# Row maxima written into score banks by ScalarE, and a new division of denominators, rotation and output projection, in a one-core macaron block

## The chip, the core and the metric

The kernel runs on one core of a Trainium2 chip. The metric is the device time of one execution in microseconds (us). The core's engines run side by side and wait for one another by semaphores: TensorE (PE, with its weight loads PEld), VectorE (DVE), ScalarE (ACT), GpSimd (POOL) and SyncE (SP), whose queue issues the DMAs here. Matmuls write to PSUM, of which the kernel uses eight banks of 128 x 512 fp32 numbers; everything else lies in SBUF or in device memory.

## What is computed

Three residual steps on x of 4 x 1024 tokens and 128 features:

```python
x = x + 0.5 * ffn(layernorm(x))      # 8 routed experts of width 128, silu(gate) * up
x = x + attn(layernorm(x))           # attn has its own layernorm and its own residual
x = x + 0.5 * ffn(layernorm(x))
```

The change lies in the attention, which has 16 heads of 64 and goes through latents of 64 numbers:

```python
c_q, c_kv = h @ w_down_q.T, h @ w_down_kv.T
q, k, v = heads(c_q @ w_up_q.T), heads(c_kv @ w_up_k.T), heads(c_kv @ w_up_v.T)
q, k = rope(q), rope(k)              # even' = even*cos - odd*sin, odd' = even*sin + odd*cos
attn = softmax(q @ k.T / 8)          # over 1024 keys, for 4 batches and 16 heads
out = concat_heads(attn @ v) @ w_out.T + residual
```

## The kernel before, in words

**Units, groups and slots.** Two heads are worked on together, one (hh = 0) in rows 0 to 63 of the PE array and one (hh = 1) in rows 64 to 127; the two form two streams of matmuls that run side by side. A unit U is one pair of heads, one half of the queries (512) and all 1024 keys, which are 8 slots of 128 keys. There are 64 units or 512 slots. The program walks over them in 128 groups g of four slots, so a unit is an even group and the odd one after it, a "pair" below.

**What a group does on PE.** First come the rows: `rows(hh)` yields for each stream 16 score matmuls (`score`, L781) and, between them, three of the four matmuls of the maxima (`passA`, L755) at the steps that `MAXIMA` lists, stream 0 first and stream 1 second. They are written alternately, one of each stream. After the rows follow the side work and the fourth maximum (before the side work in stream 1, after it in stream 0). In even groups the side work is the rotation's matmuls (L647, three in each stream), in odd groups the output projection (L839, four in each stream). Even groups then have the denominator of the unit before (`den`, L816). Last come the values of the four slots of the group before (`values`, L804, 16 column-split matmuls into psC).

**Scores.** Operands are kept in two parts (a rounded one and its remainder), so a slot of one stream takes three matmuls. A fourth, the row matmul, multiplies a row of ones by `maxr`, one row of negated row maxima, and so subtracts the maximum of every query. ACT then writes exp(0.125 x) into p (L785), and POOL sums the p of a unit into acc (L797). The last p of a unit can be left out of acc; `direct(U)` says how many, and `den` multiplies these with ones on PE as parts of their own, besides the part that acc is. It copies the bank to dsb (L818, ACT), which goes through device memory to dT.

**Banks.** psA[0] and psA[1] take the maxima of the two streams, psC the values. The scores go through psS[0..3] and psX in turn: slot s of stream hh uses number (2 (s mod 4) + hh) mod 5. The rotation and the output projection use psX and psS[3]; `den` and the layernorm's transposes take psS[0] and psS[1] by `aux`.

**Maxima.** A maximum's matmul runs 15 slots ahead of its use and is reduced by DVE from its one bank of 128 x 512 (L756). Once 16 of a unit are there, L760 negates and joins them, and `max_row` sends them through device memory (d) into `maxr`, in the middle of the group's rows: two DMAs on SP, the second after the first has landed.

**Rotation.** `rope(..., "vector")` (L660 to L664) runs on DVE in 55 even groups: a 1024-wide product from PSUM into rt, two 512-wide products within PSUM, two 512-wide additions into eo. ACT rounds eo into hi_r in the next odd group (L672, "cast"), and POOL takes the remainder (L680).

**Output projection.** In an odd group, three groups after its denominator, `outp` multiplies osb with G (w_up_v and w_out joined) into two banks. ACT scales the first bank in place, four times 128 wide (L849); DVE adds the scaled second bank to X, four times (L852), and then the first, 512 wide (L854).

**What sets the order.** All of it is an order written out by hand: each engine runs its instructions in the order in which this program issues them, and `at(g, fn, place)` puts a step off to a later group, at "side", "mid" (in the rows) or "end". Background work (layernorm, router) fills places called `step`. `direct`, `MAXIMA` and the dictionary of the rotation's places are the planner's constants.

Of the kernel before, what the change touches and what calls it, by code (L numbers as in the profile page):

```python
# [28 lines left out]
NSLOT = B * 128  # L29
NGRP = NSLOT // 4  # L30
PBUFS = 8
MAXIMA = ((3, 8, 13), (0, 5, 10))
OTHER, VECTOR, PE, NEVER = 0, 1, 2, 3
NROPE = 9
ACTS = (4, 6, 7)
# [5 lines left out]

def direct(U):

    return 1 if U % 3 == 2 and U < 56 else 0


class Kernel:
# [10 lines left out]
    def setup(self):  # L58
# [34 lines left out]
        for hh in range(2):  # L93
            nc.gpsimd.memset(self.f(self.one_row[64 * hh:64 * hh + 1, :]), 1.0)
        self.maxr = [const.tile([128, 512], F32R, name=f"maxr{i}") for i in range(2)]
        for t in self.maxr:
            nc.gpsimd.memset(self.f(t), 0.0)

# [12 lines left out]
    def aux(self):  # L111

        self.nrest += 1
        return self.rest[(self.nrest - 1) % len(self.rest)]

    def router_weights(self):
        nc, wrf = self.nc, self.wrf
# [507 lines left out]
    def rope(self, n, stage):  # L625
# [14 lines left out]
        elif stage == "mm":  # L640
            ps = w["ps"] = self.rope_banks
            hi, lo = w["C"][:, 0, :], w["C"][:, 1, :]

            def mm(k, eo):
                wt, c = ((self.wup1, hi), (self.wup1, lo), (self.wup2, hi))[k]
                r64 = slice(64 * eo, 64 * eo + 64)
                nc.tensor.matmul(ps[eo], wt[r64, qk * 4 + g, :], c[r64, :], start=k == 0, stop=k == 2)  # L647
# [3 lines left out]
        elif stage in ("o", "e"):  # L651
            k = "eo".index(stage)
            ps = w["ps"][k].unsqueeze(1).to_broadcast([128, 2, 512])
            nc.vector.tensor_tensor(self.rt[:, 2 * k:2 * k + 2, :], ps, self.table[:, 1 - k:3 - k, cs], ALU.mult)
        elif stage == "vector":


            w["eo"] = P.tile([128, 2, 512], F32, name="eo", bufs=2)
            (even, odd), rt = w["ps"], self.rt
            nc.vector.tensor_tensor(rt[:, 0:2, :], even.unsqueeze(1).to_broadcast([128, 2, 512]), self.table[:, 1:3, cs], ALU.mult)  # L660
            nc.vector.tensor_tensor(even, odd, self.table[:, 0, cs], ALU.mult)
            nc.vector.tensor_tensor(odd, odd, self.table[:, 1, cs], ALU.mult)
            nc.vector.tensor_tensor(w["eo"][:, 1, :], odd, rt[:, 1, :], ALU.add)  # L663
            nc.vector.tensor_tensor(w["eo"][:, 0, :], even, rt[:, 0, :], ALU.add)  # L664
        elif stage == "sum":
            w["eo"] = P.tile([128, 2, 512], F32, name="eo", bufs=2)
            nc.gpsimd.tensor_tensor(w["eo"], self.rt[:, 0:2, :], self.rt[:, 2:4, :], ALU.add)  # L667
        elif stage in ("hi0", "hi1"):
            k = int(stage[2])
            if k == 0:  # L670
                w["hi"] = P.tile([128, 2, 512], F32R, name="hi_r")
            nc.scalar.copy(w["hi"][:, k, :], w["eo"][:, k, :])  # L672
        elif stage == "dhi":
            self.dma(out=scr[0:2, :, :, cs].rearrange("s h i t -> (h i) s t"), in_=w["hi"])
        elif stage in ("lo0", "lo1"):
            k = int(stage[2])
            eo = w["eo"][:, k, :]
            nc.gpsimd.tensor_tensor(eo.bitcast(F32R), eo, self.f(w["hi"][:, k, :]), ALU.subtract)
        elif stage == "lo":
            nc.gpsimd.tensor_tensor(w["eo"].bitcast(F32R), w["eo"], self.f(w["hi"]), ALU.subtract)  # L680
        elif stage == "dlo":
            self.dma(out=scr[2:4, :, :, cs].rearrange("s h i t -> (h i) s t"), in_=w["eo"])
            self.roped.add((b, g, qk, h))
            del self.rope_of[n]
# [78 lines left out]
    def max_row(self, U, m):  # L763
        nc = self.nc
        d = self.dram.tile([128, 8], F32, name=f"d3_{U % 4}")
        self.dma(out=d, in_=m)
        self.dma(out=self.maxr[U % 2][0:128:64, :].rearrange("h (q p) -> h q p", p=128), in_=d.rearrange("p (h q) -> h q p", h=2))

    def score(self, s, hh, k):

# [5 lines left out]
        ks = slice(c * 128, c * 128 + 128)  # L776
        r = slice(64 * hh, 64 * hh + 64)
        Q, K = self.QT[P % 3], self.KT[P % 3]
        ps = (self.psS + [self.psX])[(2 * (s % 4) + hh) % 5]
        w, x = ((K[r, 0, ks], Q[r, 0, qs]), (K[r, 0, ks], Q[r, 1, qs]), (K[r, 1, ks], Q[r, 0, qs]), (self.one_row[r, :], self.maxr[U % 2][r, :]))[k]  # L780
        nc.tensor.matmul(ps, w, x, start=k == 0, stop=k == 3)  # L781
        if k == 3:
            if hh == 0:
                self.p_of[s] = self.pp.tile([128, 2, 512], F32, name="p")
            nc.scalar.activation(self.p_of[s][:, hh, :], ps, AF.Exp, scale=0.125)  # L785
            if hh == 1:
                self.accumulate(s)

    def accumulate(self, s):
# [18 lines left out]
    def den(self, U):  # L808

        nc = self.nc  # L810
        osb = self.osb_of[U] = self.op2.tile([128, 512], F32, name="osb")
        pd = self.aux()
        parts = [self.p_of[8 * U + c] for c in range(8 - direct(U), 8)] + [self.acc_of[U]]
        for k, part in enumerate(parts):
            for n in range(4):
                nc.tensor.matmul(pd[32 * n:32 * n + 32, 0:256], self.ones, part[:, n // 2, 256 * (n % 2):256 * (n % 2) + 256], start=k == 0, stop=k == direct(U))  # L816
        dsb = self.op1.tile([128, 256], F32, name="dsb")
        nc.scalar.copy(dsb, pd[:, 0:256])  # L818
        dT = self.ms.tile([128, 8], F32, name="dT")
# [7 lines left out]
    def outp(self, U, osb, dT):  # L827
# [8 lines left out]

        def mm(i, hh):
            r = slice(64 * hh, 64 * hh + 64)
            nc.tensor.matmul(po[hh][:, i * 128:(i + 1) * 128], osb[r, i * 128:(i + 1) * 128], self.G[r, j, :], start=True, stop=True)  # L839

        for hh in range(2):
            self.halves[hh] += [lambda i=i, hh=hh: mm(i, hh) for i in range(4)]
# [1 line left out]
        def add():  # L844

            t0 = b * TPB + 4 * half
            for i in range(4):
                c = slice(i * 128, (i + 1) * 128)
                nc.scalar.activation(po[0][:, c], po[0][:, c], AF.Identity, scale=rT[:, i:i + 1])  # L849
            for i in range(4):  # L850
                x = self.X[:, t0 + i, :]
                nc.vector.scalar_tensor_tensor(x, po[1][:, i * 128:(i + 1) * 128], rT[:, 4 + i:5 + i], x, ALU.mult, ALU.add)  # L852
            x = self.X[:, t0:t0 + 4, :]
            nc.vector.tensor_tensor(x, po[0].rearrange("p (t d) -> p t d", t=4), x, ALU.add)  # L854

        self.at(self.group, add)

    def run(self):
# [109 lines left out]
        for _ in streams[2].pop() if streams[2] else ():  # L968
            pass
        assert not (streams[0] or streams[2])  # L970
        self.rest, self.rope_banks, self.bankO = self.psS[:2], [self.psX, self.psS[3]], [self.psX, self.psS[3]]
        streams[2] += [self.attn_pre(b) for b in range(1, B)]
        turns = {"next": 0}
        needs = {}
# [43 lines left out]
        for g in range(NGRP + 1):  # L1018
# [6 lines left out]

            def rows(hh):
                maxima = lambda i: self.passA(s0 + AHEAD + i, hh) if s0 + AHEAD + i < NSLOT else None
                for n in range(16):
                    if n in MAXIMA[hh]:
                        yield lambda n=n: maxima(MAXIMA[hh].index(n))  # L1030
                    yield lambda n=n: self.score(s0 + n // 4, hh, n % 4) if g < NGRP else None
                if hh == 1:
                    yield lambda: maxima(3)
                yield from side[hh]
# [18 lines left out]

            free = g < 16 or g % 2 == 1 or g >= 2 * (16 * B - NROPE) + 2
            step(PE if free else OTHER, free)
            if g and g % 2 == 0:
                self.den(g // 2 - 1)
            rope(g, "end")
            self.run_later(g, "end")
            if g == 1 or (g < NGRP and g % 4 == 3):  # L1060
# [9 lines left out]
            for s in range(s0 - 4, s0):  # L1070
                if s >= 0:
                    self.values(s)
                if s == s0 - 3:
                    step(VECTOR, free)
        for i in range(2):
            for k in range(2):
                for hl in range(2):
# [76 lines left out]
```

## Time and profile before

| what | value |
|---|---|
| median of 3 runs | 1653.41 us (1652.72 to 1654.09) |
| the profiled execution: span from its first to its last instruction | 1648.4 us |
| the median beyond this span | 5.0 us |
| mean granted clock of TensorE | 0.994 |
| PE / PEld busy | 1593.2 / 1033.2 us |
| DVE / ACT / POOL busy | 1317.6 / 1013.5 / 1456.0 us |
| instructions of PE | 11044 |
| stretch of the attention with the steadiest pace | about 400 to 1310 us |

The profile is one execution. Its own time is its span, and what lies around it, 5.0 us against the median of the timed runs. An entry of the costliest groups reads: line, engine, operation, written tile <- read tiles, shapes, count, then busy time, mean duration in ns, and the engine's idle time just before these instructions with what ended most of it. In timeline lines the first number is the start and the second the time from the first start to the last end of the instructions that the line joins (x4 is four of them). Matmuls overlap: 0.39 us long, they start every 0.23 us within one stream, and the two streams run beside each other.

### The profile page before, as it was taken

How to read it: one execution, taken by the hardware profiler on the slowest of the kernel's cores; microseconds unless marked ns; L12 is line 12 of the kernel's file. 1: busy time of each engine (PE TensorE's matmuls, PEld its weight loads, DVE VectorE, ACT ScalarE, POOL GpSimd, SP SyncE). 2: the span in 40 equal slices, each digit the busy share in tenths (PEclk: the TensorE clock that was granted, in tenths of full speed). 3: DMA queues.
4: the chain of work that ended last, by engine and by line, in shares of the span. 5: the costliest groups of instructions: out<-in, count | busy, mean ns of one | idle time of the engine just before them, and what ended most of it. 6: DMA issues, size and time to landing. Idle time of an engine off the chain costs nothing.

```text
span 1648.4 us, 31237 instructions
## 1 busy us (share of the span) xinstructions
PE 1593.2 (97%) x11044; PEld 1033.2 (63%) x11044; DVE 1317.6 (80%) x2417; ACT 1013.5 (61%) x2220; POOL 1456.0 (88%) x833
## 2 busy tenths in 40 slices
PE   7998989999999999999999999999999999998998
PEld 5876765566566665666565666666566655656776
DVE  6556668888988888888899889889988868616897
ACT  4675666666666666666666656666566655654555
POOL 5668889999999989999999999999999999895676
PEclk9999999999999999999999999999999999999999
DMA  7025557555555655555555556666655532114443
GB/s 226 1 65 166 155 141 168 142 142 130 134 140 140 142 142 134 146 140 138 131 138 142 129 143 152 150 147 141 141 140 149 130 66 53 36 57 138 140 133 103
DMA packets 241149, 212.28 MB, mean 129 GB/s; under 512 B 157664, under 2 KB 170592, under 8 KB 240224
## 3 DMA queue, kind: packets, MB, share of 16 engines
q1 hardware_dynamic: 240992, 210.28, 50.6%
q8 instruction: 87, 1.43, 0.4%
q14 instruction: 70, 0.57, 0.1%
HBM read 130.39 MB, written 79.82 MB: 128 GB/s over the span
## 4 chain that ended last, share of the span: by engine, by line
PE 68%; POOL 3%; DVE 3%; ACT 2%; issue 2%; POOLq 0%; DVEq 0%; ACTq 0%
PE psc L804 24%; PE ps_s L781 21%; PE ps_a L755 6%; PE psx L781 3%; PE ps_s L521 3%; PE ps_s L816 2%; PE psx L476 2%; PE psx L839 2%; POOL acc L797 2%; PE psx L647 2%; ACT p L785 1%; PE ps_s L839 1%; POOL p L529 1%; PE psc L521 1%; DVE m L756 1%
## 5 line engine op out<-in xcount | busy, mean ns | idle before, releaser
L797 POOL TENSOR_TENSOR acc<-acc,p 128x1024 f32<-128x1024 f32 x366 | 872.6, 2384 | 56.3 <-ACT p L785 30.8
L756 DVE TENSOR_REDUCE m<-ps_a 128x1 f32<-128x512 f32 x1024 | 684.8, 688 | 158.0 <-PE ps_a L755 136.2
L785 ACT ACTIVATE p<-ps_s 128x512 f32<-128x512 f32 x896 | 478.2, 602 | 230.7 <-PE ps_s L781 197.1
L781 PE MATMUL ps_s<-QT,KT 64*128 64x512 f32 x2688 | 548.3, 397 | 3.1 <-DVE eo L663 3.0
L804 PE MATMUL psc<-p,ckn 128*64 128x512 f32 x2048 | 468.8, 600 | 0.0
L781 PEld LDWEIGHTS ps_s<-QT,KT 64*128 64x128 f32 x2688 | 351.2, 185 | 138.8 <-issue 76.3
L755 PE MATMUL ps_a<-KT,QT 64*128 64x512 f32 x1024 | 417.9, 419 | 5.0 <-DVE m L756 3.5
L804 PEld LDWEIGHTS psc<-p,ckn 128*64 128x64 f32 x2048 | 135.8, 137 | 257.3 <-issue 252.3
L781 PE MATMUL ps_s<-maxr,one_row 64*128 64x512 f32 x896 | 237.0, 391 | 0.0
L755 PEld LDWEIGHTS ps_a<-KT,QT 64*128 64x128 f32 x1024 | 184.5, 184 | 36.4 <-DVE m L756 12.8
L797 POOL TENSOR_TENSOR acc<-p 128x1024 f32<-128x1024 f32 x64 | 152.4, 2381 | 14.2 <-ACT p L785 11.9
L806 ACT COPY osb<-psc 128x512 f32<-128x512 f32 x64 | 37.6, 587 | 193.3 <-PE psc L804 193.3
L680 POOL TENSOR_TENSOR eo<-eo,hi_r 128x1024 fp32r<-128x1024 f32 x55 | 132.0, 2400 | 0.0
L781 PEld LDWEIGHTS ps_s<-maxr,one_row 64*128 64x128 f32 x896 | 122.3, 185 | 13.5
L781 PE MATMUL psx<-QT,KT 64*128 64x512 f32 x384 | 110.2, 393 | 0.0
L529 POOL TENSOR_TENSOR p<-eo,p 128x512 fp32r<-128x512 f32 x42 | 62.7, 1499 | 40.6 <-ACT p L528 33.1
L425 POOL TENSOR_TENSOR X<-X,dtmp 128x512 f32<-128x512 f32 x54 | 69.1, 1280 | 32.1 <-ACT dtmp L424 31.0
L852 DVE SCALAR_TENSOR_TENSOR X<-ps_s,rT,X 128x128 f32<-128x128 f32 x248 | 68.8, 339 | 26.4 <-PE ps_s L839 26.4
L849 ACT ACTIVATE psx<-psx,rT 128x128 f32<-128x128 f32 x248 | 85.4, 344 | 6.0
L672 ACT CAST hi_r<-eo 128x512 fp32r<-128x512 f32 x128 | 72.9, 615 | 18.8 <-POOL eo L667 14.0
L785 ACT ACTIVATE p<-psx 128x512 f32<-128x512 f32 x128 | 76.9, 601 | 4.4 <-issue 2.1
L781 PEld LDWEIGHTS psx<-QT,KT 64*128 64x128 f32 x384 | 71.1, 185 | 8.5
(237 smaller groups left out, 2388.2 us busy)
## 6 DMA issues: line engine op xcount, KB each, us to landing
C_l<-cs SPq DMA_DIRECT2D x128, 256.0 KB
QT<-qs SPq DMA_DIRECT2D x256, 128.0 KB
KT<-ks SPq DMA_DIRECT2D x256, 128.0 KB
qs<-hi_r SPq DMA_DIRECT2D x32, 512.0 KB
qs<-eo SPq DMA_DIRECT2D x32, 512.0 KB
ks<-hi_r SPq DMA_DIRECT2D x32, 512.0 KB
ks<-eo SPq DMA_DIRECT2D x32, 512.0 KB
rt<-wt SPq DMA_DIRECT2D x52, 256.0 KB
```

The lines of the kernel that those rows point to most:

```text
L425: nc.gpsimd.tensor_tensor(X[:, t:t + 4, :], X[:, t:t + 4, :], tmp, ALU.add)
L529: (nc.gpsimd if m < N - 1 else nc.vector).tensor_tensor(sh[:, 1, :], hp, self.f(sh[:, 0, :]), ALU.subtract)
L672: nc.scalar.copy(w["hi"][:, k, :], w["eo"][:, k, :])
L680: nc.gpsimd.tensor_tensor(w["eo"].bitcast(F32R), w["eo"], self.f(w["hi"]), ALU.subtract)
L755: nc.tensor.matmul(self.psA[hh], self.QT[P % 3][r, 0, q0:q0 + 128], self.KT[P % 3][r, 0, kk * 512:kk * 512 + 512], start=True, stop=True)
L756: nc.vector.tensor_reduce(m[0][:, hh, qb, kk:kk + 1], self.psA[hh], AX.X, ALU.max)
L781: nc.tensor.matmul(ps, w, x, start=k == 0, stop=k == 3)
L785: nc.scalar.activation(self.p_of[s][:, hh, :], ps, AF.Exp, scale=0.125)
L797: nc.gpsimd.tensor_tensor(acc, self.p_of[s - 1] if c == 1 else acc, self.p_of[s], ALU.add)
L804: nc.tensor.matmul(self.psC[64 * hh:64 * hh + 64, :], self.ckn[b % 2][:, c, :], self.p_of[s][:, hh, :], start=c == 0, stop=c == 7)
L849: nc.scalar.activation(po[0][:, c], po[0][:, c], AF.Identity, scale=rT[:, i:i + 1])
L852: nc.vector.scalar_tensor_tensor(x, po[1][:, i * 128:(i + 1) * 128], rT[:, 4 + i:5 + i], x, ALU.mult, ALU.add)
```

## The change

- After `maxr` has landed, its row is sent to device memory (d5, at the end of the group) and in the middle of the next group broadcast to all 128 partitions of `maxb` (two DMAs, one for each stream). ACT copies `maxb` into a score bank (`fill`) where the bank's writing state allows it (`full`), and the three score matmuls then add onto what lies there; the row matmul of that slot is left out. A group's fills are for slots 0 (both streams) and 1 (stream 0), after the rows of the group before, and for slot 1 of stream 1 between its third and fourth values. A bank that `aux` handed out is not filled. `MAXIMA` is set to other steps, since such streams have 14 score matmuls.
- `direct` gives two of three units below 56 one direct part, and the last unit three. `den` runs between the second and the third values, on psA[0] in place of an `aux` bank.
- The rotation on DVE is two 1024-wide products from PSUM into rt and one 1024-wide addition of two halves of rt. Its two banks change places.
- The output projection's additions are eight DVE operations of 128 columns; ACT's scaling goes.

The counts by the order of instructions on the engines: the 1024 row matmuls become 549, the denominators' matmuls go from 328 to 428 as the program issues them, 475 copies of ACT are new, its 256 scalings go, POOL has 25 sums less, and SP issues 64 + 128 more DMAs.

```diff
...
 PBUFS = 8
-MAXIMA = ((3, 8, 13), (0, 5, 10))
+MAXIMA = ((2, 6, 11), (0, 4, 9))
 OTHER, VECTOR, PE, NEVER = 0, 1, 2, 3
 NROPE = 9
 ACTS = (4, 6, 7)
...
-    return 1 if U % 3 == 2 and U < 56 else 0
+    if U == 2 * 8 * B - 1:
+        return 3
+    return 1 if (U % 3 > 0 if U < 56 else U % 3 == 2) else 0
...
 class Kernel:
...
         self.maxr = [const.tile([128, 512], F32R, name=f"maxr{i}") for i in range(2)]
+        self.maxb = [const.tile([128, 2, 512], F32, name=f"maxb{i}") for i in range(2)]
+        self.full, self.filled, self.maxb_of = set(), set(), set()
         for t in self.maxr:
...
         self.nrest += 1
-        return self.rest[(self.nrest - 1) % len(self.rest)]
+        bank = self.rest[(self.nrest - 1) % len(self.rest)]
+        self.full.discard(id(bank))
+        return bank
...
         nc, wrf = self.nc, self.wrf
...
             def mm(k, eo):
+                self.full.add(id(ps[eo]))
                 wt, c = ((self.wup1, hi), (self.wup1, lo), (self.wup2, hi))[k]
                 r64 = slice(64 * eo, 64 * eo + 64)
                 nc.tensor.matmul(ps[eo], wt[r64, qk * 4 + g, :], c[r64, :], start=k == 0, stop=k == 2)
...
             (even, odd), rt = w["ps"], self.rt
-            nc.vector.tensor_tensor(rt[:, 0:2, :], even.unsqueeze(1).to_broadcast([128, 2, 512]), self.table[:, 1:3, cs], ALU.mult)
-            nc.vector.tensor_tensor(even, odd, self.table[:, 0, cs], ALU.mult)
-            nc.vector.tensor_tensor(odd, odd, self.table[:, 1, cs], ALU.mult)
-            nc.vector.tensor_tensor(w["eo"][:, 1, :], odd, rt[:, 1, :], ALU.add)
-            nc.vector.tensor_tensor(w["eo"][:, 0, :], even, rt[:, 0, :], ALU.add)
+            for k, src in enumerate((even, odd)):
+                nc.vector.tensor_tensor(rt[:, 2 * k:2 * k + 2, :], src.unsqueeze(1).to_broadcast([128, 2, 512]), self.table[:, 1 - k:3 - k, cs], ALU.mult)
+            nc.vector.tensor_tensor(w["eo"], rt[:, 0:2, :], rt[:, 2:4, :], ALU.add)
         elif stage == "sum":
             w["eo"] = P.tile([128, 2, 512], F32, name="eo", bufs=2)
             nc.gpsimd.tensor_tensor(w["eo"], self.rt[:, 0:2, :], self.rt[:, 2:4, :], ALU.add)
...
         self.dma(out=d, in_=m)
-        self.dma(out=self.maxr[U % 2][0:128:64, :].rearrange("h (q p) -> h q p", p=128), in_=d.rearrange("p (h q) -> h q p", h=2))
+        row = self.maxr[U % 2]
+        self.dma(out=row[0:128:64, :].rearrange("h (q p) -> h q p", p=128), in_=d.rearrange("p (h q) -> h q p", h=2))
+        d5 = self.dram.tile([2, 512], F32, name=f"d5_{U % 4}")
+        self.at(self.group, lambda: self.dma(out=d5, in_=row[0:128:64, :]))
+        self.at(self.group + 1, lambda: self.spread(U, d5), "mid")
+
+    def spread(self, U, rows):
+        for hh in range(2):
+            self.nc.sync.dma_start(out=self.maxb[U % 2][:, hh, :], in_=rows[hh:hh + 1, :].to_broadcast([128, 512]))
+        self.maxb_of.add(U)
+
+    def bank_of(self, s, hh):
+        return (self.psS + [self.psX])[(2 * (s % 4) + hh) % 5]
+
+    def fill(self, s, hh):
+        bank, U = self.bank_of(s, hh), s // 8
+        if s < NSLOT and id(bank) in self.full and U in self.maxb_of:
+            self.nc.scalar.copy(bank, self.maxb[U % 2][:, hh, :])
+            self.filled.add((s, hh))
...
         Q, K = self.QT[P % 3], self.KT[P % 3]
-        ps = (self.psS + [self.psX])[(2 * (s % 4) + hh) % 5]
+        ps = self.bank_of(s, hh)
+        filled = (s, hh) in self.filled
+        last = 2 if filled else 3
         w, x = ((K[r, 0, ks], Q[r, 0, qs]), (K[r, 0, ks], Q[r, 1, qs]), (K[r, 1, ks], Q[r, 0, qs]), (self.one_row[r, :], self.maxr[U % 2][r, :]))[k]
-        nc.tensor.matmul(ps, w, x, start=k == 0, stop=k == 3)
-        if k == 3:
-            if hh == 0:
+        nc.tensor.matmul(ps, w, x, start=k == 0 and not filled, stop=k == last, skip_group_check=filled)
+        if k == last:
+            self.full.add(id(ps))
+            second = s in self.p_of
+            if not second:
                 self.p_of[s] = self.pp.tile([128, 2, 512], F32, name="p")
             nc.scalar.activation(self.p_of[s][:, hh, :], ps, AF.Exp, scale=0.125)
-            if hh == 1:
+            if second:
                 self.accumulate(s)
 
     def accumulate(self, s):
...
         osb = self.osb_of[U] = self.op2.tile([128, 512], F32, name="osb")
-        pd = self.aux()
+        pd = self.psA[0]
         parts = [self.p_of[8 * U + c] for c in range(8 - direct(U), 8)] + [self.acc_of[U]]
         for k, part in enumerate(parts):
             for n in range(4):
-                nc.tensor.matmul(pd[32 * n:32 * n + 32, 0:256], self.ones, part[:, n // 2, 256 * (n % 2):256 * (n % 2) + 256], start=k == 0, stop=k == direct(U))
+                nc.tensor.matmul(pd[32 * n:32 * n + 32, 0:256], self.ones, part[:, n // 2, 256 * (n % 2):256 * (n % 2) + 256], start=k == 0, stop=k == len(parts) - 1)
         dsb = self.op1.tile([128, 256], F32, name="dsb")
         nc.scalar.copy(dsb, pd[:, 0:256])
         dT = self.ms.tile([128, 8], F32, name="dT")
...
             r = slice(64 * hh, 64 * hh + 64)
-            nc.tensor.matmul(po[hh][:, i * 128:(i + 1) * 128], osb[r, i * 128:(i + 1) * 128], self.G[r, j, :], start=True, stop=True)
+            self.full.add(id(po[hh]))
+            nc.tensor.matmul(po[hh][:, i * 128:(i + 1) * 128], osb[r, i * 128:(i + 1) * 128], self.G[r, j, :], start=i == 0, stop=True, skip_group_check=i > 0)
...
             self.halves[hh] += [lambda i=i, hh=hh: mm(i, hh) for i in range(4)]
...
             t0 = b * TPB + 4 * half
-            for i in range(4):
-                c = slice(i * 128, (i + 1) * 128)
-                nc.scalar.activation(po[0][:, c], po[0][:, c], AF.Identity, scale=rT[:, i:i + 1])
-            for i in range(4):
-                x = self.X[:, t0 + i, :]
-                nc.vector.scalar_tensor_tensor(x, po[1][:, i * 128:(i + 1) * 128], rT[:, 4 + i:5 + i], x, ALU.mult, ALU.add)
-            x = self.X[:, t0:t0 + 4, :]
-            nc.vector.tensor_tensor(x, po[0].rearrange("p (t d) -> p t d", t=4), x, ALU.add)
+            for hh in (1, 0):
+                for i in range(4):
+                    x = self.X[:, t0 + i, :]
+                    nc.vector.scalar_tensor_tensor(x, po[hh][:, i * 128:(i + 1) * 128], rT[:, 4 * hh + i:4 * hh + i + 1], x, ALU.mult, ALU.add)
...
         assert not (streams[0] or streams[2])
-        self.rest, self.rope_banks, self.bankO = self.psS[:2], [self.psX, self.psS[3]], [self.psX, self.psS[3]]
+        self.rest, self.rope_banks, self.bankO = self.psS[:2], [self.psS[3], self.psX], [self.psX, self.psS[3]]
         streams[2] += [self.attn_pre(b) for b in range(1, B)]
         turns = {"next": 0}
         needs = {}
...
                 maxima = lambda i: self.passA(s0 + AHEAD + i, hh) if s0 + AHEAD + i < NSLOT else None
-                for n in range(16):
+                steps = [(s, k) for s in range(s0, s0 + 4) for k in range(3 if (s, hh) in self.filled else 4)]
+                for n, (s, k) in enumerate(steps):
                     if n in MAXIMA[hh]:
                         yield lambda n=n: maxima(MAXIMA[hh].index(n))
-                    yield lambda n=n: self.score(s0 + n // 4, hh, n % 4) if g < NGRP else None
+                    yield lambda s=s, k=k: self.score(s, hh, k) if g < NGRP else None
                 if hh == 1:
                     yield lambda: maxima(3)
                 yield from side[hh]
...
             step(PE if free else OTHER, free)
-            if g and g % 2 == 0:
-                self.den(g // 2 - 1)
+            for t in range(3):
+                self.fill(s0 + 4 + t // 2, t % 2)
             rope(g, "end")
             self.run_later(g, "end")
             if g == 1 or (g < NGRP and g % 4 == 3):
...
                     step(VECTOR, free)
+                    if g and g % 2 == 0:
+                        self.den(g // 2 - 1)
+                if s == s0 - 2:
+                    self.fill(s0 + 5, 1)
         for i in range(2):
             for k in range(2):
                 for hl in range(2):
...
-    nc = bacc.Bacc("TRN2", target_bir_lowering=False, num_devices=1)
+    nc = bacc.Bacc("TRN2", target_bir_lowering=False, num_devices=1, dynamic_dma_scratch_size=1024)

```

## Prediction

> **What bounds the kernel now.** I read the page first: the chain of work that ended last is 68% PE, and PE is busy 97%. But PE isn't alone, which the windows view of the steady stretch shows (its columns: stretch, length, then busy time and instructions of PE, PEld, DVE, ACT, POOL):
>
> ```profile
> PE 1593.2 (97%) x11044; PEld 1033.2 (63%) x11044; DVE 1317.6 (80%) x2417; ACT 1013.5 (61%) x2220; POOL 1456.0 (88%) x833
> L781 PE MATMUL ps_s<-maxr,one_row 64*128 64x512 f32 x896 | 237.0, 391 | 0.0
> L797 POOL TENSOR_TENSOR acc<-acc,p 128x1024 f32<-128x1024 f32 x366 | 872.6, 2384 | 56.3 <-ACT p L785 30.8
> L806 ACT COPY osb<-psc 128x512 f32<-128x512 f32 x64 | 37.6, 587 | 193.3 <-PE psc L804 193.3
> ```
> ```profile
> 400.00:1310.00 910.00, 905.56 (x6792) 553.33 (x6790) 798.38 (x1444) 580.50 (x1238) 861.06 (x392) 1.00 0.58 140
> ```
>
> PE idles 4.4 us of 910, POOL 49, DVE 112, ACT 330. So PE's queue sets the pace, with POOL and DVE close behind. The timeline of an odd group (415.19 to 424.49) and of an even one (424.49 to 434.17) gives the unit of account. PE takes 9.30 in an odd group, 9.69 in an even one (10.12 where its denominator has two parts, as at 462.64). The timeline of the even group, PE and then DVE (start, duration, what), shows how tightly the two meet:
>
> ```profile
> 424.49 0.50 PE L755 MATMUL ps_a<-KT,QT 64*128 64x512 f32 x1
> 424.83 0.62 PE L781 MATMUL ps_s<-QT,KT 64*128 64x512 f32 x4
> 425.29 0.39 PE L755 MATMUL ps_a<-KT,QT 64*128 64x512 f32 x1
> ```
> ```profile
> 425.06 1.35 DVE L756 TENSOR_REDUCE m<-ps_a 128x1 f32<-128x512 f32 x2
> ...
> 429.46 1.35 DVE L756 TENSOR_REDUCE m<-ps_a 128x1 f32<-128x512 f32 x2 [0.26 <-PE psx L647]
> 430.73 1.21 DVE L660 TENSOR_TENSOR rt<-psx,table 128x1024 f32<-128x1024 f32 x1
> 432.05 0.70 DVE L661 TENSOR_TENSOR psx<-ps_s,table 128x512 f32<-128x512 f32 x1
> 432.66 0.69 DVE L662 TENSOR_TENSOR ps_s<-ps_s,table 128x512 f32<-128x512 f32 x1
> 433.44 0.69 DVE L663 TENSOR_TENSOR eo<-ps_s,rt 128x512 f32<-128x512 f32 x1
> 434.04 0.68 DVE L664 TENSOR_TENSOR eo<-psx,rt 128x512 f32<-128x512 f32 x1
> ```
>
> The rotation ends at 434.72; the next group's first maximum is in psA at 434.17 + 0.57 = 434.74. DVE is just in time today. Whatever lengthens its chain in an even group is paid by PE, since psA has one bank per stream.
>
> **Score rows.** The order of instructions shows 475 of the 1024 row matmuls gone; 93 of the 126 groups lose two of 16 in each stream. A stream's steps lie 0.23 apart (425.29, 425.52, ...), so a group gains 2 x 0.23 = 0.46. But MAXIMA moves too. The second maximum of stream 0 now stands at step 6, the seventh thing in its queue: 0.34 + 6 x 0.23 = 1.72 after the group's start. It wants psA[0], whose reduce ends at 425.06 + 1.35 - 424.49 = 1.92 (today it stands at 2.20 and waits for nothing). Stream 0 stalls 0.20 to the next step, I take 0.23. **Net -0.23 a group.** Bounds: -0.46 (no stall) to 0. The 33 groups where `aux` took two banks keep five row matmuls in a stream; I give them back 0.23 each, +7.6.
>
> **Fills.** No row shows a ScalarE copy from SBUF to PSUM. The nearest are L806, 0.59 from PSUM to SBUF, and L672, 0.615 within SBUF; I take 0.6, bounds 0.49 (spacing) and 0.62. 475 x 0.6 = 285 us, less 256 x 0.344 = 88 of L849: +197 on ACT, whose waits for the values alone are 193 us and whose idle time in the steady stretch is 330. A group's three fills follow its last exponential and have the values (3.58 us) as cover: 1.8 us. The fourth stands after the third value; the rotation reads its bank S3 first now, so it is free 1.32 after the rotation's start, and the score that adds onto it comes 1 us into the next group. Cost nothing, if the broadcast row is there; if not, see rival C.
>
> **Denominators.** 25 more parts go from POOL to PE. At 468.58, 469.04 and 469.58 a part takes 0.43 to 0.46. Two of three even groups have two parts now, not one of three. Between the second and third values PE also changes its array shape once more, 0.14 by the gap there between denominator and values. Even groups on PE: 9.69 - 0.23 + 0.14 = 9.60, and 10.03 with two parts; mean 9.89 (before 9.83). POOL loses 25 x 2.38 = 60 us, which pays for what the add below blocks there. The bank is now psA[0]: its last reduce ends near 6.1, before the step at about 7.1, and the copy to dsb (0.37) frees it near 8.4, with the next maximum of stream 0 wanting it at 9.60 + 0.80; the cover is 2 us. The DMA of dsb leaves about 1 us later on SP, with the output projection three groups (28 us) off. Nothing for both.
>
> **Rotation.** Today 1 + 4 operations span 430.73 to 434.72, each with at most one SBUF input. Now two of 1.32 (spacing of L660), then one 1024-wide add of two SBUF operands, 1.22 alone by size. What that add meets is in this trace, in an operation off this path: the router's L355, also two SBUF operands, 512 wide. Source view, tile view, timeline:
>
> ```profile
> L355 DVE TENSOR_TENSOR g<-ex,below x8: 682/1282/2218, 27.0 to 1578.2; 128x512 f32<-128x512 f32 x8
> ```
> ```profile
> L797 POOL TENSOR_TENSOR acc<-acc,p x366: 2337/2378/2727, 228.9 to 1484.8; 128x1024 f32<-128x1024 f32 x183
> ```
> ```profile
> 836.45 7.62 POOL L797 TENSOR_TENSOR acc<-acc,p 128x1024 f32<-128x1024 f32 x3
> ...
> 839.84 1.98 DVE L355 TENSOR_TENSOR g<-ex,below 128x512 f32<-128x512 f32 x1
> ```
>
> Alone it takes 0.68; beside POOL's sums 1.98, 2.22 and 1.91 (839.84, 1135.11, 1367.18): 1.2 to 1.5 more. It seems to wait until POOL's running sum ends. POOL starts one every 2.44 us, so the new add waits w, anywhere from 0 to 2.44. The last reduce ends 6.32 into the group, now 6.32 - 0.23 = 6.09; the rotation starts 0.08 before that, the add at 6.01 + 2.64 = 8.65; it ends at 9.87 + w, and the odd group's reciprocal takes 0.1. The next maximum stands ready at 9.60 + 0.57 = 10.17, or 10.60. So PE is late if **w exceeds 0.20 (one part) or 0.63 (two)**. With w even over 0 to 2.44 the mean lateness is (2.24 x 2.24)/4.88 = 1.03 and (1.81 x 1.81)/4.88 = 0.67; weighted 1:2, 0.79. Bounds: 0 (w always small) to 2.24. An average pair takes 19.73 (44 pairs, 424.49 to 1292.61) where undisturbed ones would take 19.13; half of that 0.60 I take as standing in even groups, where a late DVE is covered: -0.3. So +0.06 + 0.79 - 0.3 = **+0.55 a pair**.
>
> The Trainium skill speaks against this part of the change: "SBUF — State Buffer", section "Who interferes with whom", says a VectorE instruction with two SBUF inputs contends with a GpSimd one that reads SBUF, and the later of the two is blocked entirely. L355's rows agree; if the rule did not hold for this add, rival A's 1643 would stand in place of the sum. Its "TensorEngine Tiling (Array Packing)", section "Tiling Modes", says that a mode switch drains TensorE; the 0.14 above is what that is worth here.
>
> **Output projection.** Four ACT scales and one DVE add (0.69) become four more DVE operations at 0.277 spacing: +0.42 on DVE in odd groups, where it has 9.30 - 8.38 = 0.9 idle and no rotation. psX comes free at the end of these eight, 2.2 after their start, and is wanted by the third slot of the next group, some 3 us later. Nothing; if that cover is gone, 0.4 a pair. **End.** POOL's last sums are three fewer, so this wait goes:
>
> ```profile
> 1487.18 1.08 PE L816 MATMUL ps_s<-acc,ones 128*32 128x256 f32 x8 [5.89 <-POOL acc L797]
> 1488.19 4.77 PE L804 MATMUL psc<-p,ckn 128*64 128x512 f32 x16
> ```
>
> -5.9, -1.1 (these values take 3.65 elsewhere), +1.3 for three parts: -5.7.
>
> **Sum.** Odd groups 64 x -0.23 = -14.7; 55 even groups with a rotation +30.3; +7.6; -5.7: +17.5. The profiled span 1648.4 + 17.5 = 1665.9; the median lies 5.0 above that span, so 1670.9, **1670**.
>
> **Rivals.**
> - A, the other side: the add mostly finds POOL between sums (w below 0.20 or 0.63). POOL follows the exponentials, so its phase could be fixed to the group; against it, POOL idles 5% and drifts. Even groups then cost +0.06 x 55 = 3; sum -10, 1643.
> - B: no stall at psA[0] (the reduces run ahead, or the 0.20 is absorbed by stream 1): another -0.23 in each of about 119 groups, sum -10, 1643. Both A and B: 1616.
> - C: the broadcast comes late. The row's path was two DMAs (d at 1018.91, maxr at 1022.07, 3.16 later), now four in series, and each waits on SP with the loads and dT queued behind it:
>
> ```profile
> SPq L56 <- DMA d<-m: 158.1, 64, 4.5
> ```
> The second link leaves 4.6 into the even group (SP's maxr<-d at 429.08). At 3 to 4 us a link and with the broadcasts issued in the middle of the next group (9.7 + about 3), they land 14.5 to 17 into the pair; the first fill can use them at about 15.3. A fill that waits holds ACT, and behind it dsb (so psA[0]), the casts and the next exponentials. One late by 2.5 or more costs 0.5 to 1 us a pair: 1702 to 1734.
> - The change doesn't do what it says: the row matmuls are gone in the order of instructions, so this can only be C.
>
> **Chances.** Forecast 0.43, A 0.18, B 0.14, A and B 0.09, C 0.09, all cancelling near 1653 0.07. Faster 0.41, same 0.07, slower 0.52 (0.2%, 3.3 us, is about what can be told from no change). The range goes from 1622 (above A and B together) to 1702 (the foot of C); the forecast's own is 1658 to 1690 (w's mean and the 0.3 each off by half).
>
> **What would show it.** The add beside POOL: 2 to 3 us against 1.2 alone, and the next group's first reduce later than 0.57 after PE's start. PE waits "<-DVE m" in the rows of stream 0 (3.5 us in all before). Odd groups 9.07, even ones 10.4 or more. Fills of 0.6 with no DMA as releaser. I am wrong if even groups stay under 9.9 (A), odd ones come to 8.84 (B), or ACT waits for maxb (C).

## The result, and the profile after

The changed kernel takes 1768.82 us (median of 4 runs, 1764.72 to 1776.9) beside 1653.07 of the kernel before: 1.0711 times as long, 95% interval 1.0681 to 1.0741. The forecast was 1670, the range ended at 1702. The direction held; the size was nearly seven times too small (17 us forecast, 116 measured).

The profiled execution spans 1775.1 us. Five lines of its page answer to those shown of before:

```profile
PE 1647.3 (93%) x10769; PEld 996.0 (56%) x10769; DVE 1381.3 (78%) x2499; ACT 1187.8 (67%) x2439; POOL 1416.4 (80%) x808
L824 POOL TENSOR_TENSOR acc<-acc,p 128x1024 f32<-128x1024 f32 x341 | 823.4, 2415 | 110.0 <-ACT p L812 87.6
L806 PE MATMUL ps_s<-QT,KT 64*128 64x512 f32 x2688 | 589.4, 422 | 58.1 <-ACT ps_s L789 57.8
L789 ACT COPY ps_s<-maxb 128x512 f32<-128x512 f32 x475 | 266.4, 597 | 129.6 <-DMA maxb<-d 122.1
L669 DVE TENSOR_TENSOR eo<-rt 128x1024 f32<-128x1024 f32 x55 | 143.9, 2616 | 4.8
```

The row matmuls did go, and a fill takes the 0.6 us that was estimated (597 ns). But no engine is full: the shares of PE, DVE and POOL fell, and ScalarE, with 475 copies more, stands at 67%. Something is waited for. The columns after the second bar name it. Score matmuls idled on fills (L789), and fills on a DMA, the broadcast `maxb<-d`. The view of the waits says the same as a chain (us in total, times, longest):

```profile
PEld ps_s L806 <- ACT ps_s L789: 152.7, 145, 3.1
...
ACT ps_s L789 <- DMA maxb<-d: 122.1, 49, 6.3
```

The timeline shows one such wait. SP's queue first (start, duration):

```profile
985.26 0.57 SPq L58 DMA_DIRECT2D maxr<-d  x1
985.93 3.61 SPq L58 DMA_DIRECT2D ks<-eo  x1
989.59 2.83 SPq L58 DMA_DIRECT2D KT<-ks  x4
992.52 0.54 SPq L58 DMA_DIRECT2D d<-maxr  x1
993.11 0.52 SPq L849 DMA_DIRECT2D d<-dsb  x1
993.67 1.85 SPq L58 DMA_DIRECT2D QT<-qs  x4
995.62 2.39 SPq L780 DMA_DIRECT2D maxb<-d  x2
```

and ScalarE in the same stretch:

```profile
994.31 1.76 ACT L812 ACTIVATE p<-ps_s 128x512 f32<-128x512 f32 x3
996.64 0.78 ACT L604 ACTIVATE hT_a<-ps_s,lnsb 128x512 f32<-128x512 f32 x1 [0.57 <-PE ps_s L602]
1002.87 0.59 ACT L789 COPY ps_s<-maxb 128x512 f32<-128x512 f32 x1 [5.45 <-DMA maxb<-d]
```

and PE, when this fill is done:

```profile
1003.51 0.50 PE L806 MATMUL ps_s<-QT,KT 64*128 64x512 f32 x1 [2.67 <-ACT ps_s L789]
```

The odd group began at 990.42. Its exponentials end at 996.07 and ScalarE is free for the fills from 997.42; the broadcast lands 7 us after its issue. Until 1002.87 ScalarE stands, and the first filled slots of the next group, which begins at 1000.12, wait with it. Between 400 and 1310 us (45 pairs before, 41 after) even groups rise in the mean from 9.88 (10.24 with two parts) to 11.24 (11.76), odd ones from 9.73 to 10.30.

### The profile page after: what moved, and what is told of

Same layout as the page of the kernel before. It is cut to its first block, busy times and chain, and to the rows that moved or that the text cites. A ratio compares the mean times of both kernels' runs of the same rounds, so it can differ in the third digit from the quotient of the medians.

```text
span 1775.1 us, 31219 instructions
## 1 busy us (share of the span) xinstructions
PE 1647.3 (93%) x10769; PEld 996.0 (56%) x10769; DVE 1381.3 (78%) x2499; ACT 1187.8 (67%) x2439; POOL 1416.4 (80%) x808
## 5 line engine op out<-in xcount | busy, mean ns | idle before, releaser
L824 POOL TENSOR_TENSOR acc<-acc,p 128x1024 f32<-128x1024 f32 x341 | 823.4, 2415 | 110.0 <-ACT p L812 87.6
L761 DVE TENSOR_REDUCE m<-ps_a 128x1 f32<-128x512 f32 x1024 | 667.7, 684 | 246.3 <-PE ps_a L760 188.2
L806 PE MATMUL ps_s<-QT,KT 64*128 64x512 f32 x2688 | 589.4, 422 | 58.1 <-ACT ps_s L789 57.8
L806 PEld LDWEIGHTS ps_s<-QT,KT 64*128 64x128 f32 x2688 | 361.7, 193 | 230.4 <-ACT ps_s L789 152.7
L831 PE MATMUL psc<-p,ckn 128*64 128x512 f32 x2048 | 481.8, 602 | 0.0
L760 PE MATMUL ps_a<-KT,QT 64*128 64x512 f32 x1024 | 438.9, 450 | 32.6 <-DVE m L761 30.9
L789 ACT COPY ps_s<-maxb 128x512 f32<-128x512 f32 x475 | 266.4, 597 | 129.6 <-DMA maxb<-d 122.1
L669 DVE TENSOR_TENSOR eo<-rt 128x1024 f32<-128x1024 f32 x55 | 143.9, 2616 | 4.8
L806 PE MATMUL ps_s<-maxr,one_row 64*128 64x512 f32 x421 | 122.0, 402 | 0.0
L806 PE MATMUL psx<-QT,KT 64*128 64x512 f32 x384 | 120.5, 422 | 0.0
```

The costliest lines, as they stand in the source:

```text
L669: nc.vector.tensor_tensor(w["eo"], rt[:, 0:2, :], rt[:, 2:4, :], ALU.add)
L760: nc.tensor.matmul(self.psA[hh], self.QT[P % 3][r, 0, q0:q0 + 128], self.KT[P % 3][r, 0, kk * 512:kk * 512 + 512], start=True, stop=True)
L761: nc.vector.tensor_reduce(m[0][:, hh, qb, kk:kk + 1], self.psA[hh], AX.X, ALU.max)
L789: self.nc.scalar.copy(bank, self.maxb[U % 2][:, hh, :])
L806: nc.tensor.matmul(ps, w, x, start=k == 0 and not filled, stop=k == last, skip_group_check=filled)
L824: nc.gpsimd.tensor_tensor(acc, self.p_of[s - 1] if c == 1 else acc, self.p_of[s], ALU.add)
```

## The experiments

Theory L: the broadcast lands too late, and a waiting fill holds ScalarE and the score banks. Theory K: the rotation's new addition, which waits for GpSimd, sets the pace. Theory T: the added DMA bytes and 475 copies load the engines by themselves. The last line of the diff, a smaller scratch space for DMAs, stays in all runs. The ratios below are to the kernel before on the same chip, with 95% intervals.

**1. Fills that never wait.** The fills read a tile that no DMA writes:

```diff
+        nc.gpsimd.memset(self.maxb[0], -2000.0)
-            ...dma_start(out=self.maxb[U % 2][:, hh, :], in_=rows...)
+            ...dma_start(out=self.maxb[1][:, hh, :], in_=rows...)
-            self.nc.scalar.copy(bank, self.maxb[U % 2][:, hh, :])
+            self.nc.scalar.copy(bank, self.maxb[0][:, hh, :])
```

> The changed kernel, but the fills copy a tile that is set once to -2000 and the broadcasts go on, all into the other tile: the DMA traffic, the 475 copies and everything else stay, only the wait of a fill for its broadcast is gone (the maximum that is subtracted in the filled slots is not the row's own). Theory L, the late broadcast holds ScalarE and through it the score banks: 1650 to 1690, and VectorE's lateness after the rotation's add is all that is left above 1640. Theory K, the rotation's add blocked by GpSimd sets the pace: above 1730. Theory T, the added traffic and the 475 copies themselves load ScalarE and the DMA engines: above 1740.

Measured 1691.42 (1.0236, 1.0216 to 1.0257): 1 us above the band of L. **77 us of the 116 are the wait for the broadcast.** Bytes and copies are all still there, so T is not the main cause. The filled slots subtract a wrong maximum here and in runs 5 and 9, so other numbers pass through the engines; run 7 tries L with the right ones. The fills' own line no longer names a DMA:

```profile
L790 ACT COPY ps_s<-maxb 128x512 f32<-128x512 f32 x475 | 266.1, 602 | 16.2 <-DVE X L879 14.4
```

**2. No fills at all.** d5 and `spread` left out, `MAXIMA` as before:

```diff
-        self.at(self.group, lambda: self.dma(out=d5, in_=row[0:128:64, :]))
-        self.at(self.group + 1, lambda: self.spread(U, d5), "mid")
-MAXIMA = ((2, 6, 11), (0, 4, 9))
+MAXIMA = ((3, 8, 13), (0, 5, 10))
```

> The changed kernel without fills and broadcasts (every slot has its row matmul again, MAXIMA as before the change); denominators, rotation and output projection stay as changed. Theory L: near 1680, that is before plus 55 pairs of about 0.6 us for the rotation's add and the second direct part, less 6 at the end. Theory K: above 1730. Theory T: near 1680 as well.

Measured 1692.30 (1.0243, 1.0226 to 1.0259). The rest of the change costs 41 us alone, 12 more than L forecast, and with it in place fills that never wait are worth nothing (1691.4 beside 1692.3).

**3. A shorter way for the row.** The first DMA writes the maxima in the order of the row, and row and broadcast are both read from there:

```diff
+        d = self.dram.tile([2, 512], F32, name=f"d3_{U % 4}")
+        self.dma(out=d.rearrange("h (q p) -> p h q", p=128), in_=m.rearrange("p (h q) -> p h q", h=2))
+        self.dma(out=self.maxr[U % 2][0:128:64, :], in_=d)
+        self.spread(U, d)
```

> The changed kernel with a shorter way for the maxima: the first DMA writes them to device memory in the order of the row, and both the row maxr and the broadcast maxb are read from there at once, in the even group, instead of after maxr and d5 in the next group. The same fills and the same bytes, less one DMA a unit. Theory L: within 15 of the run with the constant fill, 1650 to 1690. Theory K: above 1730. Theory T: above 1740.

Measured 1866.88 (1.1302, 1.1283 to 1.1321): much slower, and K and T can't say why: add and copies are the same, the bytes hardly less. The wait of SP's queue for this first DMA was 158.1 us over 64 in the kernel before. Here it is

```profile
SPq L58 <- DMA d<-m: 633.7, 64, 15.1
```

so 1024 pieces of 4 bytes written to device memory take 9.9 us to be waited for, against 2.5 in rows of 32 bytes. Where a fill waited, the broadcast landed 22.5 us into the pair instead of 20.3. The run failed as a cure, and it doesn't isolate L: its fills wait 142.2 us for the broadcast, only 20 more than in the changed kernel, while it is 98 us slower. SP's queue stands during the 9.9 us, all that is queued behind stands with it, and PE now waits for the rotation's latents, of which the view of the changed kernel has no such row:

```profile
PE ps_s L654 <- DMA C_l<-cs: 38.9, 21, 3.0
```

The Trainium skill bears on the long write ("DMA: Bandwidth & Descriptors", section "Specifications"): below 512 bytes a transfer becomes a read-modify-write. Both forms lie below that, and here eight times as many pieces of an eighth of the size still made a factor of four; no run separates number from size.

**4. The same with the rotation's five operations of before.**

> As the run with the short way, and the rotation on VectorE in its five operations of before, none with two SBUF operands. If the add's wait for GpSimd costs what was predicted (0.79 - 0.3 a pair plus what the psA[0] stall leaves), 25 to 45 faster than the short way alone: 1620 to 1650. If the add is covered, within 8 of it. Theory K: back to 1650 whatever the fills do.

Measured 1862.72 (1.1285, 1.1251 to 1.1319), 4 us less, which is not clear of the noise. While the broadcast is this late, the add costs next to nothing: the two don't add.

**5 and 6. The old rotation where no fill waits.** It goes into runs 1 and 2.

> As the run with the constant fill (1691), with the rotation's five VectorE operations of before. What is left above before in that run is put down to the rotation's add (odd groups 10.26 long where undisturbed ones take 9.11, their first reduce 1.6 to 2.0 after PE's start). If that holds: 55 odd groups lose about 0.8 each or more, 1635 to 1655. If the rest comes from the denominators, MAXIMA or the output projection: above 1675.

> As the run without fills (1692), with the rotation's five operations of before: only the denominators and the output projection are still changed. If the add is the cause: 1650 to 1668 (25 second parts at 0.43 are 11 us, less 6 at the end). If the denominators or the output projection are: above 1675.

Measured 1669.62 (1.0099, 1.0070 to 1.0128) and 1657.39 (1.0025, 1.0010 to 1.0039). Without fills the add is worth 34.9 us, and denominators and output projection together 4 (by the interval 1.7 to 6.4; the scratch space is in this run too). With fills the add seems worth 22, and the time lies above the 1635 to 1655 that was expected. Run 5's waits show why, and run 9 changes the two rotation banks back to their old order:

```diff
-        self.rest, self.rope_banks, ... = self.psS[:2], [self.psS[3], self.psX], ...
+        self.rest, self.rope_banks, ... = self.psS[:2], [self.psX, self.psS[3]], ...
```

> As the run with the constant fill and the old rotation (1669.6), with the rotation's two banks in the order of before. In that run the fourth fill waited 81 us in all for the rotation's last addition, since psS[3] was then the operand read last; with psX and psS[3] changed back it is read one operation earlier (0.69) and written by no other. If that wait is what the old rotation still cost: 1640 to 1655, and the rotation's add is worth 35 to 50 in the run with the constant fill. If the fills cost in another way: 1665 or more.

Runs 5 and 9, waits:

```profile
ACT ps_s L792 <- DVE eo L672: 81.3, 54, 3.7
```
```profile
ACT ps_s L792 <- DVE eo L671: 51.5, 54, 3.1
```

Measured 1663.47 (1.0067, 1.0052 to 1.0082). The fourth fill waits for the rotation's last reader of psS[3]; 30 us less of it go with 6 in the time, though the intervals of the two runs overlap. So the add costs 22 us beside fills, 28 with the banks' new order (1691.4 to 1663.5). The time is above the band of 1640 to 1655; 11 us remain where the forecast without the add has a gain of some 10 (rival A's 1643).

**How the add is late.** One pair of run 1: DVE, then POOL, then PE.

```profile
649.81 1.21 DVE L669 TENSOR_TENSOR rt<-psx,table 128x1024 f32<-128x1024 f32 x1
651.12 3.15 DVE L670 TENSOR_TENSOR eo<-rt 128x1024 f32<-128x1024 f32 x1
654.19 0.19 DVE L863 RECIPROCAL rT<-dT 128x8 f32<-128x8 f32 x1
654.31 2.51 DVE L762 TENSOR_REDUCE m<-ps_a 128x1 f32<-128x512 f32 x4
```
```profile
648.37 4.81 POOL L825 TENSOR_TENSOR acc<-acc,p 128x1024 f32<-128x1024 f32 x2
653.15 2.00 POOL L243 TENSOR_TENSOR rstdf<-rstdf,neghalf 128x4 f32<-128x4 f32 x1
```
```profile
654.99 0.49 PE L761 MATMUL ps_a<-KT,QT 64*128 64x512 f32 x1 [0.65 <-DVE m L762]
```

The add takes 3.15; the shortest of the 55 takes 1.225, the median 3.08. It ends about one undisturbed length after POOL's second sum does (653.18), and POOL's next operation, four numbers wide, lasts 2.00 where its shortest took 1.01. The odd group began at 652.69; its first reduce starts 1.62 later in place of 0.57, and PE waits. In the mean of the odd groups between 400 and 1300 us this first reduce starts 1.38 after PE in run 1, 0.57 in the kernel before.

**7 and 8. The broadcast a group earlier.** Four more maxima in each stream in group 4, all later ones four slots further ahead, `maxr` three deep; run 8 also has the old rotation and old `direct`.

```diff
+                lead = s0 + AHEAD + (4 if g > 4 else 0)
+                maxima = lambda i: self.passA(lead + i, hh) if lead + i < NSLOT else None
+                if g == 4:
+                    for i in range(4, 8):
+                        yield lambda i=i: maxima(i)
```

> The changed kernel with its maxima four slots further ahead from group 5 on (group 4 makes eight instead of four in each stream) and a third maxr tile: the row is sent and broadcast one group earlier, by the same four DMAs, with the same bytes, fills and rotation. Late broadcast: near the run with the constant fill, 1680 to 1705. If ScalarE's wait had another cause than the broadcast's time of arrival: above 1740.

> As the run with the maxima further ahead, with the rotation's five operations of before and one direct part in every third unit as before (the last unit none): a version meant to keep what the fills gain. An undisturbed pair is 9.11 + 9.68 (10.11 in one of three) where before takes 9.30 + 9.69 (10.12): 0.2 a pair, 13 us, so 1635 to 1650 if nothing else waits; above 1660 if the broadcasts are still late or the psA[0] stall takes the gain.

Measured 1708.07 (1.0334, 1.0301 to 1.0367): 61 us gained by an earlier arrival (with the third `maxr` that it needs), near run 1 but above the band. Fills wait 3.4 us for broadcasts in place of 122.1. L is shown a second time, with real broadcasts. Run 8 measured 1693.56 (1.0256, 1.0211 to 1.0300), a miss: undisturbed groups came out as expected (9.12 and 9.65), but others took up to 14.5. Its fills wait 84.3 us for the rotation's last addition, as in run 5, and in the longest group the rotation's latents were late:

```profile
581.69 0.56 SPq L58 DMA_DIRECT2D maxr<-d  x1
582.29 4.01 SPq L58 DMA_DIRECT2D C_l<-cs  x2
```
```profile
588.57 0.50 PE L654 MATMUL ps_s<-C_l,wup 64*128 64x512 f32 x1 [1.42 <-DMA C_l<-cs]
```

Whatever stands behind `maxr` in SP's queue is held some 3 us: in run 8 the latents, in the changed kernel `ks<-eo` (3.61 above).

**10 and 11. The maxima's DMAs behind the latents' fetch,** banks as before, no fills for units 0 to 3, three direct parts at the end; run 11 also sets MAXIMA to ((2, 7, 12), (0, 5, 10)).

```diff
-            self.at(self.group, lambda: self.max_row(U, m8), "mid")
+            self.at(self.group, lambda: self.max_row(U, m8))
-        self.at(self.group, lambda: self.dma(out=d5, ...))
-        self.at(self.group + 1, lambda: self.spread(U, d5), "mid")
+        self.at(self.group + 1, lambda: self.dma(out=d5, ...), "mid")
+        self.at(self.group + 1, lambda: self.spread(U, d5))
```

> As the run further ahead with the old rotation and direct parts (1693.6), with the two banks as before, the maxima's DMAs put behind the fetch of the rotation's latents (at the group's end; d5 in the middle and the broadcast at the end of the next group), no fills for units 0 to 3, and three direct parts in the last unit. In that run PE waited up to 1.9 us for the latents, whose DMA stood 4 us behind maxr's, and ScalarE for the rotation. If these two are its whole loss: odd groups 9.12, even ones 9.65 to 10.1, 1630 to 1648, faster than before. If PE's stalls come back elsewhere: 1655 or more.

> As the run with the fetch first, with the maxima one step later: ((2, 7, 12), (0, 5, 10)). An undisturbed odd group took 9.12 where two score matmuls less should give 9.30 - 0.46 = 8.84. If stalls at psA take the 0.28, and the places cause them: up to 0.28 a group less, 5 to 35 faster than the run with the fetch first. If a bank's own turn (matmul, reduce, release) sets it: the same within 5.

Measured 1696.21 (1.0268, 1.0254 to 1.0281) and 1691.71 (1.0232, 1.0215 to 1.0250): misses. Now fills wait 78 us for broadcasts that leave 7 us later in the pair than in run 8. An undisturbed odd group takes 9.11 in run 10 and 9.05 in run 11, not 8.84: with the maxima a step later most of the 0.28 stays, which speaks for a bank's own turn.

**12 and 13. Fills for odd groups only,** with real broadcasts, the old rotation, banks and direct parts. Run 13 puts `spread` at the group's end.

```diff
-        if s < NSLOT and id(bank) in self.full and U in self.maxb_of:
+        if s < NSLOT and s // 4 % 2 and id(bank) in self.full and U in self.maxb_of:
-MAXIMA = ((2, 6, 11), (0, 4, 9))
+MAXIMA = (((3, 8, 13), (0, 5, 10)), ((2, 6, 11), (0, 4, 9)))
```

> A version meant to keep what the runs leave of the gain: the changed kernel with its real broadcasts, but fills only for odd groups, which want the broadcast a whole group (some 10 us) later; even groups have all their row matmuls and the MAXIMA of before, the rotation its five operations and its banks of before, and one direct part in every third unit (three in the last). Late broadcast as the main cause: a fill is wanted about 25 into the pair where the broadcast landed at 20, so no fill waits for it. Odd groups 9.54 in the mean as with the constant fill, even ones 10.0 (10.43 with two parts) as without fills: 19.68 a pair beside 19.73 before, less 6 at the end, 1642 to 1653. If fills lose in other ways than by late broadcasts: 1658 or more.

> As the run with fills for odd groups only (1658.5), with the broadcast issued at the end of the next group, behind the fetch of the rotation's latents and the loads, in place of its middle, ahead of them. In that run no fill waited for a broadcast, odd groups took 9.11 undisturbed, and what was lost lay in a few even groups of 11 to 17, where the rotation's matmuls waited for latents queued behind the broadcast. If that queueing is the rest of the loss: 1640 to 1653, at or below before. If even groups are long for another reason: within 4 of 1658.

Measured 1658.49 (1.0039, 1.0024 to 1.0054) and 1659.52 (1.0038, 1.0021 to 1.0055): the nearest to before of the runs with fills, and 0.4% slower. In run 12 no fill waits for a broadcast. Undisturbed odd groups take 9.11 for 9.30, even ones 9.84 for 9.69, where the denominator's new place and bank are what is still changed: 0.04 a pair is left. Against that stand groups like this one, where latents issued behind the broadcast come late:

```profile
566.38 1.84 SPq L782 DMA_DIRECT2D maxb<-d  x2
568.26 0.44 SPq L853 DMA_DIRECT2D dT<-d  x1
568.74 1.44 SPq L58 DMA_DIRECT2D C_l<-cs  x2
```
```profile
574.12 0.47 PE L654 MATMUL psx<-C_l,wup 64*128 64x512 f32 x1 [1.54 <-DMA C_l<-cs]
```

Run 13 moves the broadcast behind them. Fills then wait 41.3 us for it, and the time is the same. The waits of PE and PEld for latents did not fall either (10.2 us in run 12, 11.8 here). So the queueing behind the broadcast is real, but by the run's own forecast it isn't the rest of the loss; what makes these few even groups long stays open.

## Why the prediction was wrong

- **The failed step** is "Cost nothing, if the broadcast row is there". The row was not there. Rival C had this mechanism whole, ScalarE held and the next exponentials with it, but at a chance of 0.09 and 0.5 to 1 us a pair. It cost 77 us, 1.2 a pair. Behind it stands the path of the row. The forecast put the landing at 14.5 to 17 into the pair and the need at 15.3. Of 41 units between 400 and 1310 us a fill waited in 22, and there the row landed at 20.3 in the mean, 17.4 at the earliest. The path in these 22: d at 2.3, maxr 5.3, d5 12.0, broadcast issued 15.1, its second half out by 16.0, landing 4.3 later. The link from maxr to d5 takes 6.7, not "3 to 4 us"; that figure came from the link from d to maxr in the trace of before (3.16; 2.87 in the mean of 64), which takes 3.0 here. The prediction has "the loads and dT queued behind"; the trace has loads ahead. In 21 of the 22 units, as in the queue shown above, four loads of KT stand ahead of d5 and four of QT ahead of the broadcast. None of the 19 units without a wait has them there; their link takes 5.0 and their broadcast is issued at 13.7. So the wait comes in about every second pair. The 19 also follow a wait, which makes their even group 13.05 long in place of 10.33 and their need later; how much each of the two does is open, since no run moved the loads alone.
- **What the trace of before had of it.** The two estimates, landing and need, overlapped; that was a reason to give C most of the chance. And the hold behind `maxr` stood there already, behind the `maxr` of 1022.07:

```profile
1024.37 1.55 SPq L822 DMA_DIRECT2D d<-dsb  x1
```

  This issue, 0.55 elsewhere, ends 3.85 after that of `maxr` began. In the kernel before, `d<-dsb` takes the hold, and after the change, with `den` later, `ks<-eo` or `qs<-eo` does, with the row's next link behind them.
- **The rotation's add** was forecast at 0.79 less 0.3, or 0.49 a pair: 27 us (the 0.55 also has the 0.06 of PE's other terms). It measured 22 beside fills, 28 with the banks' order, and 35 without fills. The reason held, and the size with it: the wait w was 1.38 in the mean of run 1 (adds of 2.60 less 1.225; median 1.85), where 1.22 was taken, and the odd group's first reduce came 0.81 later than before (1.38 for 0.57), where 0.79 was worked out. The rule of the Trainium skill ("SBUF — State Buffer", section "Who interferes with whom"), that the later of the two is blocked entirely, agrees with the 3.15 and the 2.00 in the pair of run 1; rival A, w mostly small, is refuted.
- **The score rows**: -0.23 forecast for an odd group, -0.19 measured (9.11 for 9.30). The psA stall is real: in an undisturbed odd group of the changed kernel the weight load for the second maximum of stream 0 idles 0.30 until DVE's reduce, 1.88 after the start. Rival B is refuted.
- **Even groups on PE**: 9.60 and 10.03 forecast, 9.66 and 10.11 undisturbed. The denominator's new place, with its extra change of array shape, is 0.15 (9.84 for 9.69 in run 12; 0.14 forecast).
- **Denominators, projection, end**: 4 us together in run 6. The prediction's terms give some 10: 0.14 for the change of shape and a third of 0.43 for the added parts are 0.28 a pair, over 55 pairs, less 5.7 at the end.
- **The fills' net gain** without any late broadcast did not come. From run 6 to run 9 odd groups go from 9.73 to 9.50 in the mean, even ones from 10.28 to 10.53. Fills still wait 51.5 us for the rotation's hold on psS[3] in run 9, and PE and PEld some 12 for late latents; what each costs, and what the 33 groups with uneven streams cost (they keep five row matmuls in both streams together, not in one), is open, since none of these runs removed them alone.
- **The sum as measured**: 77 for the late broadcast where the forecast had nothing, 28 for the add and the banks' order where it had 27, and 11 for the rest where it had a gain of 10: 116 in place of 17.

## What to carry to other kernels

When a new path of DMAs must meet a deadline, add up every link from the trace, with what stands ahead of it in its queue, and compare the end with the deadline; if the two ranges overlap, take the wait as the likely case and price it with all that is queued behind the waiting instruction. An engine with 330 us of idle time isn't cover for work that comes at one fixed moment. Taking work from the engine that sets the pace gains less than its price where a one-deep buffer ties it to a neighbour: here two matmuls less a stream were worth 0.19 of 0.46 us.

## What the runs showed of the hardware

A DMA of 1024 pieces of 4 bytes (`maxr<-d`) delays the next DMA on its queue: that one's issue ends some 3.9 us after the first began, in the kernel before (3.94 in the median of 58 `d<-dsb`) as after (3.94 and 3.95 of `qs<-eo` and `ks<-eo`, 51 together). Right behind `maxr` these issues of 512 KB take 3.3, elsewhere 0.4. Writing 1024 such pieces is waited for 9.9 us, four times as long as the same bytes in 128 rows of 32. And the mean granted clock of TensorE was lower in the runs in which fills waited longer for the broadcast: 0.994 before, 0.984 in run 10 (78 us of wait), 0.975 after (122), 0.955 in run 3 (142). Whether the waits lower it, and what that adds to the time, no run separates.
